# Order of two engines' reads in the q and k tails, and two lots of value products in place of three, in a fused attention and feed-forward block

## The chip, the cores and the metric

The kernel runs on one core of a Trainium2 chip. The metric is device time in microseconds (us) of one execution. One execution was also taken with the hardware profiler; durations below come from it.

## The reference

The input is 16 batches of 512 tokens with 512 channels, in fp32. Two sublayers follow each other, and each has a layer norm ahead of it, a layer norm behind it and a residual sum:

```
x = x + layernorm(attention(layernorm(x)))
x = x + layernorm(ffn(layernorm(x)))
```

Attention has 32 heads of 16 channels. q and k (a product with a weight, plus a bias) are turned by a rotary embedding, `y * cos + rotate_half(y) * sin`; scores are scaled by 1/4, masked causally, and put through a softmax; the weights are applied to v, and an output product follows. The feed-forward part is `silu(x Wg * gs) * (x Wu * us)` with 1408 inner channels and ternary weights, a product with Wd, and a scale.

## The kernel before

**Names.** PE is TensorE (matmul), DVE is VectorE, ACT is ScalarE, POOL is GpSimd, SP issues the DMAs. All instructions go through one helper that keeps each engine's queue in the order of the program (line 54, which is why all rows of the profile read L54). Groups of the profile are told apart by their tiles.

**Steps.** A batch's 32 heads are eight groups of four; a group takes five steps (`one_step`, line 814), so a batch is 40 steps. "Step 2.3" below means group 2 of the batch, step 3. Each step begins with score matmuls (`scores`, line 592) into `sc`, four PSUM banks that every step uses again, so the scores of the next step wait until this step's readers of `sc` are through:

- step 0: transposed scores of one key block (512 queries); ACT then takes exp of all of it into `pa` (`weights`, line 649)
- step 1: plain scores of two query blocks of the next group; DVE adds the mask and takes two maxima into `nm` (`maxima`, line 623)
- step 2: transposed scores of two key blocks; exp into `pa`; `pm`, a PE transpose of the maxima, follows and is split by ACT (`nmh`) and DVE (`nml`)
- step 3: plain scores of one query block of the group after next; mask and one maximum
- step 4: transposed scores of one key block beside plain scores of one query block; exp into `pc`, and then, on the same banks, mask and maximum

POOL zeroes the upper triangle of the exps (`affine_select`).

**Dense work.** Behind its scores each step gets a share of the "dense" list, which holds the projections and the feed-forward part of neighbouring batches: `pv`, `pq`, `po`, `px` (transposes), `pk`, `pg`/`pu` (gate and up), `pd` (down). `run_list` (line 704) cuts the list by SHARES (line 41), one weight for each of the five steps, and prefers a cut that does not lie right behind the end of a block. Dense results go to three PSUM banks in turn (`ps_d`, line 93; `pm` takes one of them too): the fourth block waits until the first one's readers are done. In groups 0 to 4 of a batch come v, then four q blocks, four o blocks, and four k blocks with the `xntf` transposes between; gate, up and down take the rest.

**A q or k block** (`qk_block`, line 352) is four fp32 matmuls, each recorded as two instructions, into one bank `p`. Its tail (lines 357 to 364) reads the bank twice: ACT copies the two halves, swapped, with the bias into `ys` (two instructions), and DVE computes `ya = (p + bias) * cos`. POOL then multiplies `ys` by sin. Three matmuls later in the list comes `rest` (line 366): DVE adds `ya + ys`, ACT rounds the sum to `yh`, and POOL takes the remainder `yl = ya - yh`. `ya` and `ys` have one buffer each: the next block's `ya` waits until `yl` has read this one. The two engines that read one bank are ordered by semaphore: the second in the program waits for the first.

**Values.** `values` (line 660) multiplies the exps with v, in three lots: lot 0 at the end of step 1, lot 1 (key blocks 3 and 1, 16 instructions) at the end of step 3, lot 2 (`pc`, 8 instructions) at the end of the next group's step 0, after which ACT copies the sum out (`ot`).

**Batches.** The lists for batches 1 to 13 are alike; batch 14's has no down part and is spread over the same 40 steps, batch 15's has no q and k blocks, and batch 0 has a short list over 47 steps.

Of the kernel before, what the change touches and what calls it, by code (L numbers as in the profile page):

```python
# [13 lines left out]
ALU = mybir.AluOpType  # L14
# [12 lines left out]
NG = H // 4  # L27
# [10 lines left out]
S_SETS = [[], [(2, 384, 0), (0, 128, 384)], [], [(3, 512, 0)], [(1, 256, 256)]]  # L38
AHEAD = [0, 1, 0, 2, 2]

SHARES = [2.3, 3.1, 3.0, 2.8, 3.9]


class InOrder:
# [14 lines left out]
class Block:  # L59
# [292 lines left out]
    def qk_block(self, b, name, c):  # L352

        bias = self.col["b" + name]
        st = {}

        def tail(p):
            ya = st["a"] = self.tile([P, T], "ya", bufs=1)
            ys = st["s"] = self.tile([P, T], "ys", bufs=1)
            for h in range(2):  # L360
                i, o = slice(64 * h, 64 * h + 64), slice(64 - 64 * h, 128 - 64 * h)
                self.act.activation(ys[o, :], p[i, :], AF.Identity, bias=bias[i, c : c + 1])
            self.dve.scalar_tensor_tensor(ya, p, bias[:, c : c + 1], self.cos, ALU.add, ALU.mult)
            self.pool.tensor_tensor(ys, ys, self.sin, ALU.mult)

        def rest():
            ya, ys = st["a"], st["s"]
            self.dve.tensor_tensor(ya, ya, ys, ALU.add)
            hi, lo = st["y"] = [self.tile([P, T], n, bufs=2, dtype=FR) for n in ("yh", "yl")]
            self.act.copy(hi, ya)  # L370
            self.pool.tensor_tensor(lo, ya, hi, ALU.subtract)

        def store():
            i = (b % 2) * NC + c
            for part, y in enumerate(st["y"]):
                if name == "q":
                    d = self.qd[i][:, part, :].rearrange("(h r) t -> h r t", r=DH)
                else:
                    d = self.kd[i][part].rearrange("(h r) t -> h r t", r=DH)
                for h in range(2):  # L380
                    self.sp.dma_start(out=d[:, 8 * h : 8 * h + 8, :], in_=y[64 * h : 64 * h + 64, :].bitcast(FP))

        return self.product(
            "p" + name, NC, lambda i: self.wts[b, name, c][:, i, :], lambda i: self.xnts["a", b][:, i, :], tail
        ), rest, store
# [318 lines left out]
    def run_list(self, L, steps, first=0):  # L704
# [3 lines left out]
        total = sum(item[0] for item in L)  # L708
        weights = [SHARES[(first + s) % STEPS] for s in range(steps)]
        done, i, goal = 0.0, 0, 0.0  # L710
# [103 lines left out]
    def one_step(self, work, n, i):  # L814
        for f, args in self.todo.pop(self.step, []):
            f(*args)
        if i == 0 and n + 2 < self.B * NG:
            self.load_group(n + 2)
        self.scores(n, i)
        if i == 2 and 0 <= n + 1 < self.B * NG:  # L820
            self.turn_maxima(n + 1)
        next(work, None)
        if i == 1 and 0 <= n < self.B * NG:
            self.values(n, 0)
        if i == 3 and 0 <= n < self.B * NG:
            self.values(n, 1)
        if i == 0 and 0 <= n - 1 < self.B * NG:
            self.values(n - 1, 2)
        self.step += 1

# [242 lines left out]
```

## Time and profile before

| what | value |
|---|---|
| time, median of three runs | 3317.96 us (3315.47 to 3319.39) |
| time of the profiled execution | 3320.11 us |
| its span, first to last instruction | 3318.4 us |
| mean granted TensorE clock | 0.971 |
| busy DVE, ACT, POOL | 1963.7, 1478.7, 1306.6 us |
| busy weight load (PEld) | 1679.7 us |

In the profile, busy time is a sum over an engine's instructions, and the idle time in front of an instruction is put down to what released it ("<-"). A row of the timeline gives the start from the start of the span, the duration, the engine, the operation, the tile written and those read, and in brackets the idle time of that engine before it. A "x4" merges neighbours of one kind. PE and PEld are the two parts of TensorE.

### The profile page before, as it was taken

To read this page: it belongs to the slowest core of one execution; us is meant where nothing else is said; L and a number is where in the kernel's file an instruction comes from. 1 tells how busy PE (TensorE), PEld (TensorE's weight loads), DVE (VectorE), ACT (ScalarE), POOL (GpSimd) and SP (SyncE) were. 2 spreads that over 40 slices of the span, in tenths; PEclk is the share of its full clock that TensorE was granted. 3 is DMA by queue.
4 is the path that set the end of the run, shared out by engine and by line. 5 is a ranking of instruction groups with operands and counts; after the bars stand their busy time and mean duration, and the time that the engine had idled before them with its cause. 6 is when DMAs were issued, how large, how long until landed. Compare 5 with 4: busy or idle time off the path is not lost. (4 is left out here: it accounts for less than half of the span.)

```text
span 3318.4 us, 55663 instructions
## 1 busy us (share of the span) xinstructions
PE 3023.2 (91%) x21258; PEld 1679.7 (51%) x21258; DVE 1963.7 (59%) x2717; ACT 1478.7 (45%) x1862; POOL 1306.6 (39%) x1550
## 2 busy tenths in 40 slices
PE   6778999999989999998999999999998999889888
PEld 3233464645546464554636455464554646445456
DVE  5454666656566665656656565665656666566543
ACT  5234444444444444445444544544444444443332
POOL 4123444343444424344442534434344443333343
PEclk9879999999999999999999999999999999999899
DMA  7444534535354453534445353443535345343332
GB/s 254 152 139 128 167 124 144 167 121 189 99 161 135 146 163 122 173 113 148 142 148 161 123 172 114 139 159 123 188 101 165 130 144 170 113 141 111 116 103 72
DMA packets 271905, 471.18 MB, mean 142 GB/s; under 512 B 45920, under 2 KB 50016, under 8 KB 271200
## 3 DMA queue, kind: packets, MB, share of 16 engines
q1 hardware_dynamic: 271200, 466.49, 43.5%
q8 instruction: 171, 2.80, 0.3%
q10 hardware_dynamic: 432, 1.05, 0.1%
q14 instruction: 102, 0.84, 0.1%
HBM read 345.79 MB, written 125.30 MB: 142 GB/s over the span
## 5 line engine op out<-in xcount | busy, mean ns | idle before, releaser
L54 DVE TENSOR_REDUCE nm<-sc 128x4 f32<-128x2048 f32 (+3 forms) x512 | 751.9, 1490 | 13.2
L54 ACT ACTIVATE pa<-sc 128x2048 f32<-128x2048 f32 x256 | 480.9, 1879 | 498.5 <-PE sc L54 482.9
L54 DVE TENSOR_TENSOR sc<-sc,mask 128x512 f32<-128x512 f32 (+1 forms) x384 | 335.4, 873 | 469.0 <-PE sc L54 290.1
L54 POOL TENSOR_SCALAR_AFFINE_SELECT pa<-pa 128x512 f32<-128x512 f32 (+1 forms) x256 | 223.0, 871 | 808.9 <-ACT pa L54 808.9
L54 POOL TENSOR_TENSOR hl<-ht,hh 128x512 fp32r<-128x512 f32 (+1 forms) x192 | 230.0, 1198 | 192.3 <-ACT hh L54 166.0
L54 PE MATMUL sc<-kh,q 32*128 32x512 f32 (+3 forms) x2048 | 205.7, 391 | 108.7 <-DVE nm L54 57.9
L54 PE MATMUL pd<-wd,hl 128*128 128x512 f32 x704 | 288.1, 409 | 14.8 <-POOL hl L54 14.8
L54 PE MATMUL pg<-xntf,wf 128*128 128x512 f32 x704 | 290.1, 412 | 12.2 <-DVE ya L54 10.3
L54 PE MATMUL pd<-wd,hh 128*128 128x512 f32 x704 | 293.0, 416 | 2.2 <-ACT hh L54 2.2
L54 PE MATMUL pg<-xntfl,wf 128*128 128x512 f32 x704 | 285.7, 406 | 1.8 <-DVE xntfl L54 1.8
L54 PE MATMUL pu<-xntf,wf 128*128 128x512 f32 x704 | 282.9, 402 | 0.0
L54 PE MATMUL pu<-xntfl,wf 128*128 128x512 f32 x704 | 278.4, 395 | 0.0
L54 PE MATMUL av<-pa,v 128*32 128x512 f32 (+2 forms) x3072 | 276.8, 463 | 0.7 <-POOL pa L54 0.4
L54 ACT ACTIVATE pc<-sc 128x1024 f32<-128x1024 f32 x128 | 131.3, 1026 | 311.6 <-PE sc L54 257.4
L54 PEld LDWEIGHTS sc<-kh,q 32*128 32x128 f32 x2048 | 100.4, 186 | 324.2 <-DVE nm L54 130.8
L54 POOL TENSOR_TENSOR yl<-ya,yh 128x512 fp32r<-128x512 f32 x128 | 162.6, 1271 | 247.4 <-ACT yh L54 247.3
L54 PE MATMUL sc<-q,kh 32*128 32x512 f32 (+3 forms) x2048 | 196.1, 372 | 69.4 <-DVE nm L54 66.8
L54 PE MATMUL pk<-xnta,w 128*128 128x512 f32 x480 | 252.9, 657 | 4.2 <-DVE ya L54 3.2
L54 POOL TENSOR_TENSOR ln_rstd<-ln_ve,neghalf 128x1 f32<-128x1 f32 x256 | 147.5, 576 | 255.5 <-DVE ln_ve L54 255.2
L54 POOL TENSOR_SCALAR_AFFINE_SELECT pc<-pc 128x512 f32<-128x512 f32 x128 | 81.6, 637 | 412.9 <-ACT pc L54 412.8
L54 PE MATMUL pq<-xnta,w 128*128 128x512 f32 x480 | 238.2, 628 | 5.2 <-ACT xntf L54 4.6
L54 PE MATMUL po<-w,oc 128*128 128x512 f32 x512 | 241.3, 608 | 0.4 <-DVE ya L54 0.4
(122 smaller groups left out, 5090.7 us busy)
## 6 DMA issues: line engine op xcount, KB each, us to landing
wf<-wgs SPq DMA_DIRECT2D x352, 256.0 KB
q<-qd SPq DMA_DIRECT2D x128, 256.0 KB
kh<-kd SPq DMA_DIRECT2D x128, 256.0 KB
kl<-kd SPq DMA_DIRECT2D x128, 256.0 KB
od<-ot SPq DMA_DIRECT2D x128, 256.0 KB
w<-in_wo SPq DMA_DIRECT2D x68, 256.0 KB
xr<-in_x SPq DMA_DIRECT2D x66, 256.0 KB
w<-in_wq SPq DMA_DIRECT2D x64, 256.0 KB
```

What stands on the lines that cost most here:

```text
L54: return self.tc.keep_in_program_order(f(*args, **kwargs))
```

## The change

Three edits. In the tail of q and k blocks the DVE instruction that writes `ya` stands ahead of the two ACT copies. `values(n, 1)` moves from the end of step 3 of its group to the end of step 0 of the next group, directly ahead of `values(n - 1, 2)`. SHARES has new weights (the sum stays 15.1).

```diff
-SHARES = [2.3, 3.1, 3.0, 2.8, 3.9]
+SHARES = [1.5, 3.1, 3.0, 3.7, 3.8]
...
             ys = st["s"] = self.tile([P, T], "ys", bufs=1)
+            self.dve.scalar_tensor_tensor(ya, p, bias[:, c : c + 1], self.cos, ALU.add, ALU.mult)
             for h in range(2):
                 i, o = slice(64 * h, 64 * h + 64), slice(64 - 64 * h, 128 - 64 * h)
                 self.act.activation(ys[o, :], p[i, :], AF.Identity, bias=bias[i, c : c + 1])
-            self.dve.scalar_tensor_tensor(ya, p, bias[:, c : c + 1], self.cos, ALU.add, ALU.mult)
             self.pool.tensor_tensor(ys, ys, self.sin, ALU.mult)
...
         if i == 1 and 0 <= n < self.B * NG:
             self.values(n, 0)
-        if i == 3 and 0 <= n < self.B * NG:
-            self.values(n, 1)
         if i == 0 and 0 <= n - 1 < self.B * NG:
+            self.values(n - 1, 1)
             self.values(n - 1, 2)
```

## The prediction

> **What bounds it now.** I read the busy table first, then the list of waits, then the timeline, one batch step by step.
>
> ```profile
> PE 3023.2 (91%) x21258; PEld 1679.7 (51%) x21258; DVE 1963.7 (59%) x2717; ACT 1478.7 (45%) x1862; POOL 1306.6 (39%) x1550
> ```
>
> TensorE sets the time: 91% busy, nobody else over 59%. Its idle 295 us (3318.4 - 3023.2) is what an edit of order can move. Whom does it wait for?
>
> ```profile
> PE sc L54 <- DVE nm L54: 124.8, 125, 5.4
> PE sc L54 <- ACT pa L54: 48.5, 51, 2.7
> PE pm L54 <- DVE ya L54: 38.6, 13, 3.0
> PE pg L54 <- DVE ya L54: 10.3, 13, 0.8
> ```
>
> Scores wait for the readers of `sc`, maxima above all, and dense blocks for a bank that `ya` still reads. By step (start of a step's first score row to the next one's, means over batches 3 to 12) these waits lie nearly all in groups 1 to 4, where the q and k tails are, some 10 us a batch; groups 5 to 7 have next to none, so there a step lasts as long as its matmuls. How a tail holds a step up is seen in step 1.4 of one batch:
>
> ```profile
> 1502.75 0.68 DVE L54 TENSOR_TENSOR ya<-ya,ys 128x512 f32<-128x512 f32 x1
> 1503.46 0.62 ACT L54 CAST yh<-ya 128x512 fp32r<-128x512 f32 x1 [4.40 <-DVE ya L54]
> 1504.10 1.39 ACT L54 ACTIVATE ys<-pq,cols 64x512 f32<-64x512 f32 x2
> 1504.15 1.27 POOL L54 TENSOR_TENSOR yl<-ya,yh 128x512 fp32r<-128x512 f32 x1 [3.68 <-ACT yh L54]
> 1505.52 1.02 ACT L54 ACTIVATE pc<-sc 128x1024 f32<-128x1024 f32 x1
> 1505.58 0.75 DVE L54 SCALAR_TENSOR_TENSOR ya<-pq,cols,turn 128x512 f32<-128x512 f32 x1 [2.15 <-POOL yl L54]
> 1506.57 0.70 DVE L54 TENSOR_TENSOR sc<-sc,mask 128x512 f32<-128x512 f32 x1 [0.24 <-ACT pc L54]
> 1507.31 1.23 DVE L54 TENSOR_REDUCE nm<-sc 128x4 f32<-128x1024 f32 x1
> 1508.68 0.51 PE L54 MATMUL sc<-q,kh 32*128 32x512 f32 x4 [0.44 <-DVE nm L54]
> ```
>
> Two things to see. ACT's copies `ys` run while POOL makes the last block's `yl`, so they fill time. DVE's `ya` waits for `yl` (its buffer), not for the copies; and ACT's exp `pc`, queued behind the copies, starts the chain exp, mask, maximum that ends at the next scores.
>
> **Part 1, `ya` first.** Nothing is added: 0.75 us on DVE and 1.39 on ACT per block, in either order. What moves is a wait. In the built order of the changed program the copies wait for `ya`, no longer for the matmul, and still stand ahead of the same exp. In step 1.4 that gives: `yh` ends 1504.08, `yl` 1505.42, `ya` 1505.58 to 1506.33, copies from 1506.38 to 1507.77 (they began at 1504.10), exp, mask and maximum 2.28 us later than above. So the **hold** is 2.28 us (1506.38 - 1504.10), wherever an exp stands behind copies that wait so. Queued behind those copies on ACT are the exp, `xntf` and `yh`; DVE's mask and TensorE's scores wait for the exp, gate products for `xntf`.
>
> [...]
>
> **Part 2, values.** In a step that waits for nothing lot 1 takes 1.00 us to the next scores (`av` 1581.22, `sc` 1582.22) and lot 2 0.57 (1590.03, 1590.60). At the dense cadence of 0.43 for 512 columns (`po`, six in 2.74 with the tail) their 1024 and 512 columns need 0.86 and 0.43; 0.14 of each is start and end. One lot saves one such piece: bounds 0 and 0.14 a group, at most 128 x 0.14 = 18 us. Where the next scores wait anyway it saves nothing, so I take it in groups 4 to 7 alone, 0.6 a batch. `ot`, and `pa`'s buffer, come free one step later; exp writes that buffer only in step 2, a step on: nothing.
>
> **Part 3, shares.** Step 0 loses about one fp32 matmul (0.86) and gains lot 1, step 3 the reverse; the sum is the same. But blocks end in other steps, so the tails meet other exps. I went through the changed order by hand, from step 1.0, with the row's durations and handoffs (exp of 2048 1.88, of 1024 1.02; masks 0.70 and 1.23; maxima 2.29, 1.23, and 2.35 for the pair; add 0.68; POOL's product 1.27). Lengths before to after:
>
> Group 1: 4.24 to 3.35, 4.52 to 5.25, 4.71 to 3.85, 6.01 to 6.75, 5.80 to 7.98. Steps 1.0 to 1.2 only trade work; q1's `ya`, waiting for `yl`, stands ahead of mask 1.3 as before; 1.4 has the hold.
>
> Group 2: 4.46 to 6.82, 5.53 to 5.40, 4.71 to 3.17, 5.05 to 6.95, 4.94 to 4.65. Step 2.0 has the hold of q3's copies on the exp (2.36). In 2.3 the first transpose now falls into the step, and the second statistics of that tile now stand behind the maximum: maximum ends 3.80, statistics 4.82, POOL 5.82, `xn` 6.68, transpose 6.75, where the matmuls end at 5.0.
>
> Groups 3 and 4: 3.77 to 5.73, 4.93 to 4.95, 8.83 to 10.3, 5.06 to 4.63, 5.04 to 8.87; 6.19 to 8.45. In 3.0 k0's `ya` stands behind statistics on DVE (it ended 0.96 after the copies before), so the exp goes back 2.0. In 3.2 `pm` gets a free bank, but k2 waits for k1's copies instead of `ya`: 8.7, and the clock's 1.6 (below). In 3.4 k2's copies stand ahead of the last `xntf`, and the gate products wait 3 us. In 4.0 `yh`, k3's copies, the tanh and `yh` again stand ahead of the exp: +2.26.
>
> The clock's 1.6: in step 3.2 TensorE idles 3 us and then runs at half speed, as these rows of the batch at 1338 show (six instructions in 4.30, not 2.74). Before pays it too, in its 8.83.
>
> ```profile
> 1350.18 0.38 PE L54 MATMUL pm<-ident,nm 128*16 128x128 f32 x1 [2.96 <-DVE ya L54]
> 1350.35 4.30 PE L54 MATMUL pk<-xnta,w 128*128 128x512 f32 x6
> ...
> 1355.74 2.74 PE L54 MATMUL pk<-xnta,w 128*128 128x512 f32 x6
> ```
>
> [...]
>
> **Sum.** Groups 1 to 4.0: before 25.28 + 24.69 + 27.63 + 6.19 = 83.8, after 27.2 + 27.0 + 34.5 + 8.45 = 97.1: +13.3, less 0.6 for the lots: +12.7 a batch, x13 = 165. Batch 14 and the short list of batch 0 have eight blocks each with other alignments; each block between 0 and one hold, 0 to 18 us each; I take the middle, 9 each, as no row is nearer to one end. Batch 15 has no tails: 0 (bounds 0 and -2 for its lots). 165 + 18 = +183 on the profiled execution's 3320.1 gives 3503; the median of the runs lies 2 below it, so **3500**.
>
> **Rivals.**
> (a) Half the holds are covered: only 1.4, 2.0 and 3.0, where the copies stand directly ahead of the exp, and not the chains through `xn` (1.9), `xntf` (3.8) and 4.0 (2.3). Then 12.7 - 8.0 - 1.5 for 3.2 = 3.2 a batch, x14 = +45, and +18: 3380. For it: these chains pass three engines, and I laid them by hand. Against: each link is in the built order.
> (b) The clock: four more waits of 2 us and over (2.0, 2.3, 3.0, 3.4) each lose 1.56 too: 14 x 6.2 = 87: 3590. Waits of 1.3 to 1.5 in this trace leave the clock at full, against it.
> (c) **Faster**: freeing DVE decides. `DVE ya` waits 100.1 us for the copies (25 times) and `pm` and `pg` wait 38.6 + 10.3 for `ya`; with these gone, the half clock of 13 batches (20) and 18 for the lots, 3320 - 87 = 3233. It decides if no exp or `xntf` stands within 2.3 us behind the copies; the rows above show an exp 0.03 behind them.
> (d) The order is not what it says, the copies starting with `ya`, or gains and losses meet: 3310 to 3325. The built order speaks against it.
>
> **Chances.** Forecast 0.60, (a) 0.18, (b) 0.12, (c) 0.06, (d) 0.04. Range: from (a) to (b), 3375 to 3590, which leaves out (c), (d) and the edges of both. A difference of 0.2% (6.6 us) is about what a measurement of this kernel can tell from no change: faster 0.06, within 0.2% 0.04, slower 0.90.
>
> **What would show it.** In the profile after: `ys` preceded by an idle time of ACT put down to `DVE ya`, large in sum (about 120 blocks x 2 us = 240); `PE sc <- DVE nm` up from 124.8 and `PE sc <- ACT pa` from 48.5, together by 80 us or more; `PE pg` waiting for `xntf` and `PE px` for `xn` in groups 2 and 3; `pm <- DVE ya` gone; the copies' start 0.05 behind `ya`'s end; groups 5 to 7 shorter by 0.1 to 0.2 us a group. Wrong it is if the exp of steps 1.4 and 2.0 starts no later behind `yh` than before, 2.1 us; then (c) holds.

## The result and the profile after

The changed kernel takes 3560.2 us (median of 4 runs, 3556.2 to 3564.1) against 3318.7 for the kernel before: ratio 1.0729, 95% interval 1.0711 to 1.0748. It is slower by 242 us; the prediction said 182, in a range of 3375 to 3590. The profiled execution's span is 3562.3 us, its mean granted clock 0.936 (before 0.971).

First the busy line of the page after, to be set against the one quoted in the prediction.

```profile
PE 3118.7 (88%) x21258; PEld 1742.4 (49%) x21258; DVE 1957.4 (55%) x2717; ACT 1479.5 (42%) x1862; POOL 1305.5 (37%) x1550
```

The counts are the same and DVE, ACT and POOL are as busy as they were. TensorE's idle time went from 295.2 to 443.6 (3562.3 - 3118.7), +148.4, and the same 21258 instructions are 95.5 busier: they ran at half clock for longer (its records add up to 459 us, 195 before). The two add up to the span's 243.9. Who is waited for stands in the list of waits (us in total, times, longest):

```profile
ACT ys L54 <- DVE ya L54: 313.3, 127, 4.5
...
DVE ya L54 <- POOL yl L54: 199.5, 97, 3.9
...
PE sc L54 <- DVE nm L54: 170.9, 81, 6.6
...
PE sc L54 <- ACT pa L54: 64.1, 58, 3.7
PE pk L54 <- ACT ys L54: 61.1, 15, 4.7
...
PE pg L54 <- ACT xntf L54: 37.0, 16, 2.7
...
PE px L54 <- ACT xn L54: 27.1, 39, 1.5
```

The top row is new. Nearly every block's copies (127 of 128) now wait for `ya`, 2.5 us each, and `ya` still waits for `yl` (97 times, 82 before). Below stand those who pay: scores, k products and gate products, held by the copies, by an instruction of ACT that stands behind them, or by the maximum behind such an exp. The last row, the transposes' wait for `xn`, is not the hold's: it is 27.0 in `e2_lots` too, which has the old tail. The step that the prediction showed, 1.4, in the timeline after:

```profile
1624.68 0.62 ACT L54 CAST yh<-ya 128x512 fp32r<-128x512 f32 x1 [2.16 <-DVE ya L54]
...
1625.38 1.26 POOL L54 TENSOR_TENSOR yl<-ya,yh 128x512 fp32r<-128x512 f32 x1 [1.46 <-ACT yh L54]
...
1626.68 0.75 DVE L54 SCALAR_TENSOR_TENSOR ya<-pq,cols,turn 128x512 f32<-128x512 f32 x1 [2.03 <-POOL yl L54]
1627.46 1.39 ACT L54 ACTIVATE ys<-pq,cols 64x512 f32<-64x512 f32 x2 [2.16 <-DVE ya L54]
...
1628.88 1.02 ACT L54 ACTIVATE pc<-sc 128x1024 f32<-128x1024 f32 x1
...
1629.94 0.70 DVE L54 TENSOR_TENSOR sc<-sc,mask 128x512 f32<-128x512 f32 x1 [2.51 <-ACT pc L54]
...
1630.67 1.23 DVE L54 TENSOR_REDUCE nm<-sc 128x4 f32<-128x1024 f32 x1
...
1632.05 0.80 PE L54 MATMUL sc<-q,kh 32*128 32x512 f32 x4 [3.46 <-DVE nm L54]
```

The order of the rows is what changed: `yh`, `yl`, `ya`, copies, exp, one after the other. From `yh` to the exp `pc` it was 2.06 us before (1505.52 - 1503.46) and is 4.20 now; TensorE's wait went from 0.44 to 3.46, and its first scores take 0.80, not 0.51: half clock (0.50 granted).

By stretches the 243.8 us of the two traces divide so: the head (all up to the first group) 110.7 to 125.0, +14.3; batch 0 169.0 to 180.7, +11.7; batches 1 to 13 2554.3 to 2756.4, +202.1; batch 14 +14.6; batch 15 +1.1.

### The profile page after: what moved, and what is told of

Its sections match the earlier page's. It is cut to its first block, busy times and chain, and to the rows that moved or that the text cites. A ratio compares the mean times of both kernels' runs of the same rounds, so it can differ in the third digit from the quotient of the medians.

```text
span 3562.3 us, 55503 instructions
## 1 busy us (share of the span) xinstructions
PE 3118.7 (88%) x21258; PEld 1742.4 (49%) x21258; DVE 1957.4 (55%) x2717; ACT 1479.5 (42%) x1862; POOL 1305.5 (37%) x1550
## 4 chain that ended last, share of the span: by engine, by line
PE 56%; DVE 19%; ACT 11%; POOL 6%; issue 6%; DMA 2%; SPq 0%; POOLq 0%; DVEq 0%; ACTq 0%
PE sc L54 13%; PE pu L54 8%; PE pg L54 8%; PE pd L54 7%; DVE nm L54 6%; PE av L54 6%; PE pv L54 5%; ACT pa L54 5%; DVE ya L54 4%; DVE sc L54 4%; POOL yl L54 3%; PE po L54 3%; PE pq L54 3%; PE pk L54 2%; DVE ln_st L54 2%
## 5 line engine op out<-in xcount | busy, mean ns | idle before, releaser
L54 PE MATMUL pk<-xnta,w 128*128 128x512 f32 x480 | 278.5, 713 | 57.1 <-ACT ys L54 56.8
L54 PE MATMUL pg<-xntfl,wf 128*128 128x512 f32 x704 | 296.8, 422 | 4.6 <-DVE xntfl L54 4.6
L54 PE MATMUL sc<-q,kh 32*128 32x512 f32 (+3 forms) x2048 | 202.1, 384 | 111.7 <-DVE nm L54 110.7
L54 POOL TENSOR_TENSOR ys<-ys,turn 128x512 f32<-128x512 f32 x128 | 162.7, 1271 | 321.4 <-ACT ys L54 319.9
L54 PE MATMUL po<-w,oc 128*128 128x512 f32 x512 | 265.7, 661 | 0.0
L54 PEld LDWEIGHTS sc<-q,kh 32*128 32x128 f32 x2048 | 103.4, 190 | 290.7 <-DVE nm L54 116.8
```

What stands on the lines that cost most here:

```text
L54: return self.tc.keep_in_program_order(f(*args, **kwargs))
```

## The experiments

Theory: the hold. The copies inherit `ya`'s wait for its one buffer, and what stands behind them on ACT pays. Rivals: the lots and shares make the loss, or the two readers' order on the bank itself does. The ten kernels ran beside the kernel before (median 3317.3 to 3317.8 in the three sets of runs).

**The two halves of the change.** `e1_swap` is before with the tail's edit alone; `e2_lots` has the two other edits alone.

```diff
+            self.dve.scalar_tensor_tensor(ya, p, bias[:, c : c + 1], self.cos, ALU.add, ALU.mult)
             for h in range(2):
...
-            self.dve.scalar_tensor_tensor(ya, p, bias[:, c : c + 1], self.cos, ALU.add, ALU.mult)
```

> Before with the tail's order swapped alone (three lots, old shares). Hold theory: the copies behind ya put back the exps of steps 1.4, 2.0, 3.0 and 4.0 by about 2 us each and the bank of 3.2 by 1.4, some 10 us a batch, and the tails ahead of the batches and in batch 0 cost some 20 more: about 3480, ratio 1.05. Rival (the moved lots and the shares cost the time, the order of the pair being free): 3310 to 3330.

Measured: 3507.4, ratio 1.0570 (1.0544 to 1.0597), +190 us. The wait that carries it is there without the other edits:

```profile
ACT ys L54 <- DVE ya L54: 268.4, 127, 3.6
```

```diff
-SHARES = [2.3, 3.1, 3.0, 2.8, 3.9]
+SHARES = [1.5, 3.1, 3.0, 3.7, 3.8]
...
-        if i == 3 and 0 <= n < self.B * NG:
-            self.values(n, 1)
...
+            self.values(n - 1, 1)
```

> Before with two lots and the new shares alone, copies first as before. Hold theory: 0.6 us a batch saved by the lots and new alignments of blocks and steps, between -20 and +60: 3300 to 3380. Rival (lots and shares cost the time): 3450 or more.

Measured: 3358.5, ratio 1.0126 (1.0098 to 1.0155), +41. 190 + 41 is 231 of the 242. So the swap makes four fifths of the loss, and lots and shares lose on their own.

**The cause of the hold.** `e3_after_ya2` is the changed kernel, `e4_before_ya2` the kernel before, each with two buffers for `ya`. To make room both pack three small things; `e10_pack` is that packing alone.

```diff
-            ya = st["a"] = self.tile([P, T], "ya", bufs=1)
+            ya = st["a"] = self.tile([P, T], "ya", bufs=2)
...
-        m = self.mask = con.tile([P, 2 * P], mybir.dt.bfloat16, tag="mask", name="mask")
+        m = self.mask = con.tile([P, P], mybir.dt.bfloat16, tag="mask", name="mask")
...
-        hi, lo = [self.tile([16, P], i, bufs=1, dtype=FR) for i in ("nmh", "nml")]
+        hl = self.tile([48, P], "nmh", bufs=1, dtype=FR)
+        hi, lo = hl[0:16, :], hl[32:48, :]
...
-        s = self.tile([P, 32], "sum", bufs=2)
+        s = self.tile([P, 32], "sum", bufs=1)
```

> After with two buffers for ya, so that it no longer waits for yl; room for it by a narrower mask tile, one tile for nmh and nml, and one buffer of sum. Hold theory: of a hold of 2.28 us, 1.5 is yl and its handoffs, so six holds a batch shrink by 1.5 each, 9 us x 14: about 3430. Rival (the copies' wait for ya alone counts, yl being done by then): 3540 to 3565.

Measured: 3347.2, ratio 1.0085 (1.0055 to 1.0115). The second buffer takes 213 of the 242 back. Copies that wait for `ya` are 33, not 127 (103.4 us, not 313.3); step 1.4 lasts 5.49, not 7.96, step 2.0 4.55, not 7.10. The theory's 3430 was 83 too high: it gave the buffer 1.5 of each hold, but three quarters of the copies that waited do not wait at all any more.

> Before with two buffers for ya, room as in the run above. DVE no longer stands still for yl (176.7 us idle before ya): mask 1.3 and the bank that pm waits for come 1.3 to 1.5 us earlier each, 3 us a batch: about 3275. Rival (ya waits for the copies next, which end when yl ends): 3310 to 3320, no change.

Measured: 3311.1, ratio 0.9985 (0.9973 to 0.9997): next to nothing. The rival was right, and one row says why. In the old order `ya` comes behind the copies, and these come behind `yh` on ACT. In the prediction's rows of step 1.4 `yl` ends at 1505.42 and the copies at 1505.49, so `ya` waited for both there; with the first wait gone the second takes its place:

```profile
DVE ya L54 <- ACT ys L54: 277.8, 110, 5.8
```

> A control: before with the packing alone (one mask tile broadcast, nmh and nml in one tile, one buffer for sum), one ya buffer, old tail. Theory: the packing moves no time, 3311 to 3324, so that the runs with two ya buffers show the buffers. Rival: the mask rows read with two repeats or the shared tile shift some steps by 0.1 to 0.5, 5 to 20 us either way, and the gains of 6 and 19 would be of the packing.

Measured: 3315.1, ratio 0.9993 (0.9984 to 1.0002). The packing moves nothing that shows.

**The swap with the buffer that it needs.** `e5_swap_ya2` is before with the swap, two `ya` buffers and the packing; three lots and the old shares stay.

> Before with the swapped tail and two buffers for ya (three lots and the old shares kept; the same packing of the mask and of nmh and nml as in the run after with two buffers, and one buffer for sum). Theory: the swap's whole price is that the copies inherit ya's wait for yl. With that wait gone the copies start 0.84 behind the bank's last matmul, and this run lands at the kernel before or a little under it, 3295 to 3320 (two buffers took the changed kernel 11 below the two lots alone, and the kernel before by 6); the idle of ACT ahead of ys put down to DVE ya falls from 268 to about 100 (0.75 a block). Rival: the 0.75 + 0.09 of ya itself still stands ahead of the exp in steps 1.4, 2.0 and 4.0, and costs 3 x 0.84 x 14 = 35: 3345 to 3355.

Measured: 3298.7, ratio 0.9942 (0.9929 to 0.9956): faster than both kernels. The theory's number held, and the wait of the copies for `ya` fell further than it said, to 57.9 (33 times). The swap by itself thus costs 190 us with one buffer and gains with two (0.9942 against 0.9985). The order of the bank's two readers is not what costs; the wait that the first one brings along is.

Beside the gains (step 1.3 6.02 to 4.44, 3.2 8.84 to 6.20) it has three losses per batch, 3.0 (3.78 to 5.79), 3.1 (4.93 to 6.26) and 4.1 (5.13 to 6.04). The timeline of such a step 3.0:

```profile
1526.12 0.69 DVE L54 BATCH_NORM_STATS2 ln_st<-x 128x6 f32<-128x512 f32 x1
...
1527.13 0.74 DVE L54 SCALAR_TENSOR_TENSOR ya<-pk,cols,turn 128x512 f32<-128x512 f32 x1
...
1527.97 1.39 ACT L54 ACTIVATE ys<-pk,cols 64x512 f32<-64x512 f32 x2 [2.82 <-DVE ya L54]
...
1529.38 1.88 ACT L54 ACTIVATE pa<-sc 128x2048 f32<-128x2048 f32 x1
...
1531.31 0.45 PE L54 MATMUL sc<-kh,q 32*128 32x384 f32 x4 [1.93 <-ACT pa L54]
```

Here no buffer is short: `ya` stands in DVE's queue behind a layer norm's statistics, the copies and the exp wait for it, and the next scores wait 1.93. `e9_swap_ya2_k0` keeps the old order in this block alone.

```diff
+            late = name == "k" and c == 0
+            if not late:
+                self.dve.scalar_tensor_tensor(ya, p, bias[:, c : c + 1], self.cos, ALU.add, ALU.mult)
...
+            if late:
+                self.dve.scalar_tensor_tensor(ya, p, bias[:, c : c + 1], self.cos, ALU.add, ALU.mult)
```

> The version with the swapped tail and two ya buffers, with the old order kept in block k0 alone. Theory: what that version still loses, 2.0 in step 3.0 and 1.3 in step 3.1 of every batch, comes from k0's ya, which stands behind xntfl and the layer norm's statistics on DVE, so that the copies and the exp behind them on ACT wait 2.0 longer; with the copies first there, they run at once and the two steps go back to 3.8 and 4.9, 3.3 x 13 = 43 less: 3255 to 3270. Rival: the 2.0 is only passed on, since POOL and the later k blocks set the length of steps 3.1 to 3.3 (step 3.2 goes back from 6.2 to 8.8, with its half clock): 3290 to 3300.

Measured: 3294.7, ratio 0.9929 (0.9916 to 0.9943), the fastest of all, though its interval overlaps that of `e5_swap_ya2`. Steps 3.0 and 3.1 went back to 3.80 and 4.93 as the theory had it, but 3.2 went from 6.20 to 8.15 and 4.1 from 6.04 to 6.66: the rival's "passed on" took most of the 3.3 back, and its number held.

**The head.** `e6_swap_front` swaps only in batch 0's eight blocks, which are computed ahead of the first group (old order where `b` is not 0).

```diff
+            if b == 0:
+                self.dve.scalar_tensor_tensor(ya, p, bias[:, c : c + 1], self.cos, ALU.add, ALU.mult)
```

> Before with the tail swapped in batch 0's eight blocks alone, which are computed ahead of the first group. Theory: those tails form a ring (ya, copies, product with sin, sum, yh, yl, next ya) that has no exp in it and is lengthened by the swap by 1.6 a block; nothing later gives it back: the head is 12.7 longer, 3317.3 becomes 3328 to 3332, and batches 0 to 15 stay as they are. Rival: transfers or the first batch wait for something else anyway, and the head's 12.7 is given back in batch 0: 3315 to 3321.

Measured: 3333.3, ratio 1.0041 (1.0028 to 1.0055), +15.5. The head lasts 123.5, not 110.7 (107.7 to 110.7 in the runs with the old order), and batch 0 169.1 as before: nothing is given back. The tails' own rhythm shows it. `ya` of two neighbouring k blocks in the head, before:

```profile
58.25 0.75 DVE L54 SCALAR_TENSOR_TENSOR ya<-pk,cols,turn 128x512 f32<-128x512 f32 x1 [2.15 <-POOL yl L54]
...
63.49 0.75 DVE L54 SCALAR_TENSOR_TENSOR ya<-pk,cols,turn 128x512 f32<-128x512 f32 x1 [2.15 <-POOL yl L54]
```

and in the changed kernel:

```profile
73.72 0.75 DVE L54 SCALAR_TENSOR_TENSOR ya<-pk,cols,turn 128x512 f32<-128x512 f32 x1 [2.02 <-POOL yl L54]
...
81.09 0.75 DVE L54 SCALAR_TENSOR_TENSOR ya<-pk,cols,turn 128x512 f32<-128x512 f32 x1 [2.02 <-POOL yl L54]
```

5.24 from one to the next becomes 7.37. The tail is a ring (`yl`, next `ya`, product with sin, sum, `yh`, `yl`). Before, the copies were done while `yl` ran and the product followed `yl` at once, beside `ya`; now `ya` and then the copies stand between them, 0.75 + 1.39 = 2.14 in all. The product is not the last that the sum comes after, though: in both kernels the sum starts 1.1 us behind the product's end, behind checks of weights on DVE that belong to the head. Before, a check ran right behind `ya` (58.92); now it waits 2.09 for a cast by ACT that stands behind the copies (76.55), so this path became longer by about as much. The one buffer is the cause here too: in `e5_swap_ya2`, with the new order and two buffers, neighbouring k blocks are 5.32 apart and the head lasts 110.5.

**Lots and shares apart.** `e7_lots_old` has two lots with the old shares, `e8_shares` the new shares with three lots; both have the old tail.

> Before with two lots alone (old tail, old shares). Theory: the loss of 41 in the run with two lots and the new shares is made by the shares, which put the end of an o block and its transposes into step 2.3 and the statistics ahead of mask 2.4; the lots by themselves cost nothing and save 0.14 a group in groups that wait for nothing: 3300 to 3317, steps 0 longer by 0.9 and steps 3 shorter by 1.0. Rival: 24 instructions at the end of step 0 delay the score rows of step 1 and with them the mask and two maxima, the longest DVE chain, which groups 1 to 4 can't hide: some 0.9 x 4 x 14 = 50 more, of which step 3 gives back less: 3330 to 3365.

Measured: 3380.5, ratio 1.0192 (1.0178 to 1.0206), +63. My theory fell: the lots alone lose more than lots and shares together. The rival had the sign, but not the size (3330 to 3365) and not the place: step 1.1 is unchanged at 4.54. Much of the time is lost behind step 3, as in this step 5.3:

```profile
1631.00 0.50 PE L54 MATMUL sc<-kh,q 32*128 32x512 f32 x4
...
1631.81 0.69 DVE L54 TENSOR_TENSOR sc<-sc,mask 128x512 f32<-128x512 f32 x1
...
1632.53 2.29 DVE L54 TENSOR_REDUCE nm<-sc 128x4 f32<-128x2048 f32 x1
...
1634.87 0.39 PE L54 MATMUL sc<-kh,q 32*128 32x256 f32 x4 [0.42 <-DVE nm L54]
```

From scores through mask and maximum to the next scores it is 3.87 (3.88 and 3.89 in the means of steps 0.3, 5.3 and 7.3). With lot 1 gone step 3's matmuls end sooner than that. Step 0 grows by 0.86 in groups 1, 3, 5, 6 and 7, by 0.66 in group 2, and not in 0 and 4, where the next scores had waited before. Step 3 gives back about 0.5 in groups 0, 4 and 5, and the next scores wait 0.4; in groups 1, 2, 3 and 6 it gives back 0.1 at most, and the scores of step 4 wait 0.9 to 1.0 more than before. (In group 7 step 3 gives back 0.98, but step 4 takes 0.97 more; why, is open.) The wait `sc <- nm` went from 124.8 to 195.4, while `sc <- pa` fell from 48.5 to 15.3; TensorE's idle time in all grew by 44 and its busy time, at a lower clock (0.963, before 0.971), by 15.

> Before with the new shares alone (old tail, three lots). Theory: the shares cost what the run with both lost and somewhat more, as step 3 now has a larger share and lot 1 too: 3350 to 3400, with step 2.3 near 7 and step 2.4 near 7 as there, and steps 3 longer by 1.0 in groups 5 to 7, which step 0 gives back. Rival: the lots made the loss, and the shares alone are neutral, 3310 to 3325, with 2.3 near 5 and 2.4 near 5.

Measured: 3381.3, ratio 1.0200 (1.0186 to 1.0214), +64, as the theory had it. Group 2 is longer by 2.4 a batch (2.3 7.99, 2.4 5.94, where 7 was said of each; both were near 5.0: the first transpose falls into 2.3 and waits for `xn`), group 0 by 2.4 (0.1 6.02 for 4.61, 0.3 5.30 for 4.44). Together 13 x 4.7 = 61; the other groups gain and lose nothing in sum. So the shares do match the lots (with them, 63 becomes 41), but they move the end of the o blocks to a worse place.

## Why the prediction was right, and where it fell short

The lengths of the steps that decide, means over batches 3 to 12, in us:

| step | before | forecast | after | e1_swap | e2_lots |
|---|---|---|---|---|---|
| 1.4 | 5.91 | 7.98 | 7.96 | 7.96 | 5.93 |
| 2.0 | 4.45 | 6.82 | 7.10 | 7.08 | 4.38 |
| 2.3 | 5.05 | 6.95 | 6.99 | 5.05 | 6.99 |
| 2.4 | 5.03 | 4.65 | 6.93 | 4.96 | 6.94 |
| 3.0 | 3.78 | 5.73 | 5.56 | 5.78 | 4.44 |
| 3.2 | 8.84 | 10.3 | 10.90 | 8.76 | 8.61 |
| 3.4 | 5.06 | 8.87 | 10.00 | 5.05 | 6.42 |
| 4.0 | 6.16 | 8.45 | 6.91 | 8.35 | 6.15 |
| groups 1 to 4.0 | 84.1 | 97.1 | 99.8 | | |

**The hold**: right in kind and size. From `yh` to the exp it is 2.14 longer in step 1.4 (2.28 said). That one buffer is the cause is shown by `e3_after_ya2` and `e5_swap_ya2`, except in step 3.0, where DVE's queue makes the wait (5.55 with two buffers, 5.56 with one). That the pair itself costs the same in either order, as the prediction counts it (0.75 + 1.39), is near the truth once that inherited wait is gone: `e5_swap_ya2` is 0.4% faster than `e4_before_ya2`. One reading was too narrow: the old `ya` waited for the copies as well as for `yl` (`e4_before_ya2`). Ten of the 16 steps worked out by hand, from 1.0 to 4.0, lie within 0.13 of the measured length, and 2.0, at 0.28, and 3.0, at 0.17, near. The larger misses partly cancel, and that is luck.

**Step 2.4**, said to become shorter (4.65), is the largest miss in a batch, 2.28. The prediction put one tile's statistics behind the maximum of 2.3 and took DVE to be free after them. The timeline after:

```profile
1656.36 0.70 DVE L54 BATCH_NORM_STATS2 ln_st<-x 128x6 f32<-128x512 f32 x1 [2.27 <-POOL x L54]
...
1658.10 0.69 DVE L54 BATCH_NORM_STATS2 ln_st<-x 128x6 f32<-128x512 f32 x1
...
1659.37 0.67 DVE L54 TENSOR_TENSOR sc<-sc,mask 128x512 f32<-128x512 f32 x1
...
1661.45 0.53 PE L54 MATMUL sc<-q,kh 32*128 32x512 f32 x4 [2.15 <-DVE nm L54]
```

DVE stands 2.27 for POOL's `x`, and two statistics of different tiles then come ahead of the mask, whose exp had long ended (1655.85 + 1.00). The wait came from the lots and shares, not the swap: 6.94 in `e2_lots`, 4.96 in `e1_swap`. A wait of DVE's queue was worked out for one step and not carried into the next.

**The clock.** The prediction kept 1.6 for step 3.2 as before and put in nothing for half clock in any other step. Four stretches of the batch above are at half clock; the answer for these windows gives the stretch, its us, TensorE's busy time, the granted clock and DMA:

```profile
1631.10:1637.90 6.80, 5.86 (x28) 0.50 0.47 143
1661.80:1665.20 3.40, 3.40 (x18) 0.50 0.39 141
1675.50:1682.30 6.80, 4.75 (x6) 0.50 0.24 79
1692.50:1695.90 3.40, 3.20 (x8) 0.51 0.12 45
```

They lie behind TensorE's waits at the end of steps 1.4 (3.46) and 2.4 (2.15) and inside steps 3.2 (4.27) and 3.4 (2.66), and they do so in all ten batches of the table. Of the waits that rival (b) named, those of 2.0, 2.3, 3.0 and 3.4, only the last is among them. At half clock TensorE is busy through steps 2.0 and 3.0, up to the next scores (it waits 0.00 and 0.12 there), and 2.3's wait of 1.5 leaves the clock at full.

What a stretch costs is read from what ends last in its step.

- Step 2.0, behind the wait of 1.4: in all ten batches the step's exp ends 0.41 to 0.59 before the next scores start, so the slow matmuls set the length, and not the hold. `e1_swap` shows both cases in one trace: the step takes 6.6 in the four batches with at most 3.4 us at half clock in it, and 7.3 to 7.5 in the six with 6.4 or more. So half clock adds some 0.5 here; the hold alone stays under the 6.82 said.
- Step 3.0: the exp ends 0.05 before the next scores, and TensorE's own work no later. Half clock adds nothing.
- Step 3.2, 0.60 longer than said: TensorE is busy 4.75 us of the stretch, which loses 2.4 at half clock (an estimate), where 1.6 was put in.
- Step 3.4, 1.13 longer than said: the products follow each other after 0.42 us, not 0.23, eight of them, which is 1.5. But a wait follows that hides it, at the end of step 4.0:

```profile
1691.98 0.50 PE L54 MATMUL pg<-xntf,wf 128*128 128x512 f32 x1 [2.66 <-ACT xntf L54]
...
1693.30 0.63 PE L54 MATMUL pg<-xntf,wf 128*128 128x512 f32 x1
1693.72 0.63 PE L54 MATMUL pg<-xntfl,wf 128*128 128x512 f32 x1
...
1695.47 0.62 ACT L54 CAST yh<-ya 128x512 fp32r<-128x512 f32 x1 [2.62 <-DVE ya L54]
...
1696.37 0.40 PE L54 MATMUL pu<-xntf,wf 128*128 128x512 f32 x1
1696.60 0.40 PE L54 MATMUL pu<-xntfl,wf 128*128 128x512 f32 x1
...
1697.39 0.50 PE L54 MATMUL sc<-q,kh 32*128 32x512 f32 x4
1697.51 0.75 DVE L54 SCALAR_TENSOR_TENSOR ya<-pk,cols,turn 128x512 f32<-128x512 f32 x1 [2.07 <-POOL yl L54]
...
1698.29 1.38 ACT L54 ACTIVATE ys<-pk,cols 64x512 f32<-64x512 f32 x2 [2.20 <-DVE ya L54]
...
1702.39 1.87 ACT L54 ACTIVATE pa<-sc 128x2048 f32<-128x2048 f32 x1
...
1704.32 0.45 PE L54 MATMUL sc<-kh,q 32*128 32x384 f32 x4 [1.96 <-ACT pa L54]
```

The chain from `yh` through `yl`, `ya`, the copies, the tanh (`sg`), the sum and `yh` to the exp runs on ACT, POOL and DVE and waits for none of these products, so the scores of 4.1 come at 1704.32 with or without the 1.5. So of TensorE's 95.5 us of extra busy time only a part reaches the end: some 0.5 a batch in 2.0 and 0.8 in 3.2, 17 us in 13 batches (an estimate from these rows; only step 2.0 was seen with both clocks).

**Step 4.0** missed the other way (8.45 said, 6.91 found). The hold there is real, 8.35 with the swap alone. In the changed kernel step 3.4's wait and slow products put the first scores of 4.0 back, to 1.92 behind the `yh` at which the chain above begins; so a part of the hold lies in step 3.4. The two steps together take 16.91, for 17.32 said.

**The sum.** Groups 1 to 4.0 missed by 2.7 a batch; the rest of the batch, 112.2 before and 111.8 after, fell by 0.4 for the 0.6 said of the lots, but not where that was said: group 0 fell by 0.56, and groups 5 to 7 together grew by 0.5. The prediction's +12.7 a batch came out at 15.5 over batches 1 to 13: 202 for 165. Batch 14 and batch 0, middles of wide bounds, were 14.6 and 11.7 for 9 each. And a term was missing: the prediction puts batch 0's own eight blocks in the head at nothing, without a word. It counts a hold where an exp stands behind the copies, and there is no exp in the head, but the ring itself is the bound: 14.3. 37 + 8.3 + 14.3 + 1.1 for batch 15 is 61, the way from the 3503 said of the profiled execution to its 3564.

**What would show it.** The wait of `ys` for `ya`: 313.3 for 240. `PE sc <- DVE nm` and `<- ACT pa`: 235.0 together, +62, less than the 80 named; the rest moved to `pk <- ys` (61.1), `pg <- xntf` and `px <- xn`, the last two as named. `pm <- ya` is gone, and in its place the k product two instructions on waits for the copies: 4.27 in step 3.2. The copies start 0.03 behind `ya`'s end. One sign failed: groups 5 to 7 were to be shorter by 0.1 to 0.2 each, and went by -0.41, +0.08 and +0.81. The lots' 0.14 a group is not shown either: with the new shares group 5 takes 22.61 with three lots (`e8_shares`) and 22.46 with two (`e2_lots`), but groups 6 and 7 are longer by 0.5 with two.

**The rivals.** (c) fell: DVE no longer stands behind the copies, and yet the swap gains only with the second buffer. (a) fell: 2.3 pays in full (6.99 for 6.95), and 3.4 and 4.0 together are 5.7 longer, of the 6.1 said. (d) fell by the first row of the waits. (b) came near in TensorE's busy time (87 said, 95.5 found), but only one of its four places was right, and most of that time is hidden; by the estimate above the clock accounts for 17 of the 60 us that the forecast was short.

## What to carry to other kernels

Before changing which of two engines reads a buffer first, look at what the new first reader waits for in the trace: its wait becomes the second one's, and everything queued behind the second one pays (190 us here, and a gain of 0.4% once the wait's buffer was doubled in both orders). A chain of tails that feeds itself is a ring: where nothing else bounds, its period is the time, and work that moved from beside the ring into it was paid in full here (5.24 to 7.37). The slow clock cost time here only where TensorE's work ended last (some 0.5 us in step 2.0, nothing in step 3.0); read that from the wait that follows it. Work that is moved out of a step gains nothing once the step is as short as the chain of other engines that its next scores wait for (3.87 us for scores, mask and maximum here), so shares are matched to chains, not only to matmul counts.

## What the runs showed of the hardware

These are counts of this case: the records of the granted clock in the traces before and after, set against TensorE's idle times from 130 to 3000 us. Half clock followed waits shorter than the 2.96 us of the prediction's row: 2.15 at the end of step 2.4. In the trace of the changed kernel none of 34 idle times of TensorE from 0.6 to 1.5 us has a record of half clock that starts in it or within 1.5 us of its end, 3 of 45 from 1.5 to 2.1, 27 of 28 from 2.1 to 2.7, not the one of 2.8, and all 29 over 3.1. Length alone doesn't tell: in the trace before it is none of 89, 5 of 20, 1 of 4, 12 of 16 from 2.7 to 3.1, and the one over 3.1.

The records of half clock last 3.4 us (44 of 86 after, 20 of 37 before) or 6.8 (38 and 15), seldom longer, and in each of the two traces all start whole multiples of 3.413 us apart (to 0.002 us). Cut at these multiples from 130 to 3000 us, the two traces have 66 stretches at full clock in which TensorE is busy for less than 40%, and all 66 are followed by half clock; of 112 with 40 to 70% it is 19, and of 1366 with more none. Of the idle times of 2.1 to 2.7 us, all 27 that lie within one such stretch have a record of half clock, and 1 of the 5 that are spread over two. A record of 3.4 us costs TensorE up to 1.7 us where nothing waits afterwards (an estimate: half its length, at the granted 0.50).
